# Mamba's opening chain rearranged, and the experts' choices made chunk by chunk

## The chip, the cores and the metric

The kernel runs on one core of one Trainium2 chip. The time is device microseconds of one execution. The engines are named as in the profile: PE (TensorE), DVE (VectorE), ACT (ScalarE), POOL (GpSimd) and SP (SyncE, which only issues DMAs and loads registers). Each engine works through its own queue in order, and semaphores tie the queues together.

## The reference

The input is an image tensor of 2 x 256 x 32 x 32 in f32. Four layers follow each other.

```python
x = x + mamba_blocks(group_norm(x))      # layer 0: two Mamba blocks, 16 states, 512 inner channels
x = involution(x)                        # layer 1: 7x7 taps, two convolutions, softmax, weighted shifts
t = tokens(x)
t = t + linear_attention(layer_norm(t))  # layer 2
t = t + experts(layer_norm(t))           # 16 experts, the best 2 of each token
t = t + softmax_attention(layer_norm(t)) # layer 3
t = t + experts(layer_norm(t))
```

A Mamba block projects 256 channels to 512, convolves along the tokens with four taps per channel, and computes a step size delta = softplus(dt @ dt_w + dt_b). Then it runs, for each of 512 channels and 16 states, h = exp(delta * A) * h + delta * B * x over 1024 tokens. The sum over the states of h * C, plus D * x, is gated and projected back. In the experts' layers each token's gate logits (16) give its two best experts and their softmax weights; each expert is silu(z w1) * (z w2), times w3.

## The kernel before

There are 2048 tokens, in 4 chunks of 512 (`NCH`) and 16 tiles of 128 (`NT`). A planner orders the whole program: it takes the instructions in the order in which the Python code issues them as their priority, models each one's duration, and lets a later instruction go ahead of an earlier one on the same engine where the earlier one's inputs are not ready by its model. So the order of the Python code is a priority, not the order on the engine.

**Mamba** (`layer0`, lines 564 to 644). `GroupNorm.image` normalises one image: `bn_stats` on DVE (L207), a PE product with a block matrix that averages over the eight channels of a group (L210, L219), small DVE steps (L212 to L217), a square root on ACT (L146), and four DVE instructions that rewrite `x` (L225). `Mamba.load` loads a block's weights and makes 16 diagonal 128 x 128 matrices of the convolution's taps (L257); `load_rest` makes four more of D (L277). `Mamba.front(j)` computes what a chunk needs before its scan: PE projection (L300), PE convolution by the diagonals (L327), `xd`, `ct`, then `dt` on PE (L370) and softplus in pieces on ACT (Abs L375, Exp L383, Ln L386) and on DVE or POOL (L377 to L401). The very first front (`alone=True`) has nothing beside it and uses DVE. There are eight units (two blocks, four chunks). `scan(j)` runs 16 states. Per state, POOL multiplies `du` by a broadcast row of B (L450, two products of 128 x 1024, into six buffers `h`), ACT makes exp(delta * A) in PSUM (L457), and DVE scans (L461, four of 128 x 512). PE transposes the result (L429), and DVE adds it into `ya` (L438). The next unit's front, the rest of the last one (`back`) and the next block's loads are issued in between at paced slots, 63 to a scan (`paced`). PSUM has two banks `mm`, three `da` and three `ht`.

**Experts.** `Gate.chunk(j, psum)` is called when a chunk of four tiles has left the attention before: it normalises the tiles, writes them to DRAM (`zd`), transposes them and computes the logits (L1297, L1301). After the last chunk `route` (L1330) chooses the two best experts of all 16 tiles at once (L1348 to L1354, on 128 x 256), counts, and gives each of 2 x 2048 choices a slot in groups of 128 rows of one expert. It then makes `expert` (which expert a group belongs to, L1404), `used` (how many groups there are, L1406), and by one-hot products on PE (L1433) the inverse of the slots, `target` and `source` (L1440, L1442). `experts` loads `used` into registers (L1477). Per group, POOL gathers 128 rows of `zd` by `source` (L1484), SP reads the expert's number (L1489) and issues its weights, 1536 KB (L1491); PE multiplies (L1514, L1528), and POOL scatters the result (L1534). 38 groups always run; more run under a condition on `used`.

Of the kernel before, what the change touches and what calls it, by code (L numbers as in the profile page):

```python
# [10 lines left out]
F32 = mybir.dt.float32  # L11
I32 = mybir.dt.int32
# [7 lines left out]
P = 128  # L20
# [4 lines left out]
C = 256  # L25
# [40 lines left out]
class Net:  # L66
# [30 lines left out]
    def counters(self, const):  # L97

        nc = self.nc
        self.rows = const.tile([P, NROWS], F32, name="rows_sb")  # L100
        nc.sync.dma_start(self.rows, self.rows_dram.partition_broadcast(P))
# [38 lines left out]
    def row(self, name):  # L140
        at, w = _ROWS[name]
        return self.rows[:, at : at + w]
# [38 lines left out]
class GroupNorm:  # L181
# [18 lines left out]
    def image(self, b):  # L200
# [8 lines left out]
        ps = self.psum.tile([P, TC], F32, tag="mm", name=f"gn_ps{b}")  # L209
# [8 lines left out]
        ps = self.psum.tile([P, TC], F32, tag="mm", name=f"gn_ps2{b}")  # L218
# [11 lines left out]
class Mamba:  # L230
# [14 lines left out]
    def load(self):  # L245
# [8 lines left out]

        self.taps = wpool.tile([P, NDC * 4, P], F32, tag="taps", name=f"{m}_taps")
        for i in range(NDC * 4):
            nc.vector.tensor_scalar_mul(  # L257
                self.taps[:, i, :], net.ident, net.col(f"{m}_conv_w", i)
            )
# [3 lines left out]
        self.state = wpool.tile([P, NS, NDC], F32, tag="state", name=f"{m}_state", bufs=2)  # L263

    def load_rest(self):
# [10 lines left out]
        for dc in range(NDC):  # L276
            nc.vector.tensor_scalar_mul(self.skip[:, dc, :], net.ident, net.col(f"{m}_D", dc))  # L277
# [6 lines left out]
    def front(self, j, alone=False):  # L284
# [83 lines left out]
        for dc in range(NDC):  # L368
            ps = self.ps_mm.tile([P, TC], F32, tag="mm", name=f"{m}_dt_{j}_{dc}")
# [35 lines left out]
    def scan(self, j, before, between):  # L405
# [38 lines left out]
        for n in range(NS):  # L444
# [3 lines left out]
            for g in range(NDC // G):  # L448
                h = scanp.tile(half, F32, tag="h", name=f"{m}_h_{j}_{n}_{g}", bufs=6)
                nc.gpsimd.tensor_mul(  # L450
# [113 lines left out]
def layer0(net, x, x_dram, m1, m2, load_image, taps, conv_dram, lg):  # L564
# [5 lines left out]
    with (  # L570
# [15 lines left out]
        norm = GroupNorm(net, wpool, ps_mm, x)  # L586
        blocks[0].load()
        load_image()
# [6 lines left out]
        units = [(m, j) for m in blocks for j in range(NCH)]  # L595
        for _ in units[0][0].front(0, alone=True):
            pass
        norm.image(1)
        before, done = iter(()), []
        aside = taps.make(ps_mm, conv_dram)  # L600
        for u, (m, j) in enumerate(units):
            steps = [(b, Mamba.GATED, 0, 35) for b in done]
            fronts = []
            for a, k in units[u + 1 : u + 2]:
                if k == 0:
                    a.load()
                fronts.append(a.front(k))
            rest = m.load_rest() if u and j == 0 else iter(())
# [26 lines left out]
            before = m.scan(j, before, paced(63, steps))  # L635
# [527 lines left out]
def softmax_attention(net, t, combine, then, scores):  # L1163
# [5 lines left out]
    with (  # L1169
# [56 lines left out]
        for i in range(NT):  # L1226
# [40 lines left out]
            if i % TPC == TPC - 1:  # L1267
                then(i // TPC, ps_mm)


class Gate:


    def __init__(self, net, layer, t, gate_w, pool, dram):
# [5 lines left out]
        self.weight = pool.tile([P, 2, NT], F32, tag="weight", name=f"{layer}_weight")  # L1280
        self.yd = net.nc.dram_tensor(f"{layer}_yd", (2 * T, C), F32, kind="Internal").ap()

    def chunk(self, j, psum):
        net, nc, layer, pool = self.net, self.net.nc, self.layer, self.pool
        z = pool.tile([P, TPC, C], F32, tag="z", name=f"{layer}_z_{j}")
        tiles = [z[:, i, :] for i in range(TPC)]
        net.norm_rows(tiles, [self.t[:, j * TPC + i, :] for i in range(TPC)])
        nc.sync.dma_start(
            self.zd[j * TC : (j + 1) * TC, :].rearrange("(i p) c -> p i c", p=P), z
        )  # L1290
        zt = pool.tile([P, NCC, TC], F32, tag="gzt", name=f"{layer}_gzt_{j}", bufs=1)
        for cc in range(NCC):
            nc.scalar.copy(zt[:, cc, :], net.transposed(psum, tiles, cc, "mm"))
        ps = psum.tile([P, TC], F32, tag="mm", name=f"{layer}_g_{j}")
        for i in range(TPC):
# [6 lines left out]
            self.logits[:, j * TPC : (j + 1) * TPC, :],  # L1302
            ps[:, : TPC * NE].rearrange("p (i e) -> p i e", e=NE),
            net.row(f"{layer}_gate_b").unsqueeze(1).to_broadcast([P, TPC, NE]),
        )

# [23 lines left out]
def route(net, one, ps_mm, pr, weight):  # L1330
# [10 lines left out]
    belowb = net.below.unsqueeze(1).to_broadcast(sh)  # L1341

    hot = [one.tile(sh, F32, name=f"hot{k}") for k in range(2)]
# [363 lines left out]
```

## Time and profile before

| | us |
|---|---|
| median of 3 runs (2205.85 to 2215.26) | 2212.17 |
| the profiled execution's own time | 2216.64 |
| its span | 2214.9 |
| busy in the span: PE, DVE, ACT, POOL | 1907.6, 1416.1, 963.5, 1007.1 |

The page's strips cut the span into 40 slices of 55.4 us, one digit of busy tenths for each. A line of the timeline gives start and length in us, engine, source line, operation, the tiles written and read, and the count; square brackets hold idle time of the engine just before and what ended it. A line of the groups ends in busy us and mean ns of one, then idle us before. A line of waits reads: who waited, for whom, us in total, times, the longest.

### The profile page before, as it was taken

How to read it: one execution, taken by the hardware profiler on the slowest of the kernel's cores; microseconds unless marked ns; L12 is line 12 of the kernel's file. 1: busy time of each engine (PE TensorE's matmuls, PEld its weight loads, DVE VectorE, ACT ScalarE, POOL GpSimd, SP SyncE). 2: the span in 40 equal slices, each digit the busy share in tenths (PEclk: the TensorE clock that was granted, in tenths of full speed). 3: DMA queues.
4: the chain of work that ended last, by engine and by line, in shares of the span. 5: the costliest groups of instructions: out<-in, count | busy, mean ns of one | idle time of the engine just before them, and what ended most of it. 6: DMA issues, size and time to landing. Idle time of an engine off the chain costs nothing.

```text
span 2214.9 us, 27264 instructions
## 1 busy us (share of the span) xinstructions
PE 1907.6 (86%) x9652; PEld 1349.1 (61%) x9652; DVE 1416.1 (64%) x2184; ACT 963.5 (44%) x1611; POOL 1007.1 (45%) x688
## 2 busy tenths in 40 slices
PE   5779888798988989788999999949999599949996
PEld 2445554555555555555556555638999467649995
DVE  5999999999999989999204376662222443342223
ACT  4576765767766767754212264411111132311111
POOL 1687694968768596885024240003333000023331
PEclk8879878897998979799999999969999899969997
DMA  2121121111212111220030100027999300049998
GB/s 105 36 61 49 36 65 32 42 51 40 70 33 66 32 49 38 58 68 24 5 67 1 48 15 0 20 75 258 334 323 346 102 3 17 20 173 332 329 329 295
DMA packets 90483, 224.16 MB, mean 101 GB/s; under 512 B 35451, under 2 KB 51712, under 8 KB 79716
## 3 DMA queue, kind: packets, MB, share of 16 engines
q1 hardware_dynamic: 77620, 198.58, 26.9%
q0 software_dynamic: 7728, 19.15, 2.8%
q10 hardware_dynamic: 4992, 4.59, 0.7%
q8 instruction: 81, 1.33, 0.2%
q14 instruction: 62, 0.51, 0.1%
HBM read 204.88 MB, written 19.37 MB: 101 GB/s over the span
## 4 chain that ended last, share of the span: by engine, by line
PE 34%; DVE 23%; issue 19%; POOL 11%; ACT 8%; DMA 4%; POOLq 0%; ACTq 0%; DVEq 0%; SPq 0%
DVE m_h L461 11%; DVE m_ya L438 6%; PE acc L746 3%; POOL x L1484 3%; PE m_ht L429 3%; POOL l_yd L1534 3%; PE early_acc L746 3%; PE av L1260 3%; PE sc L1234 2%; DMA l_yd<-y,target 2%; PE h L1083 2%; ACT m_da L457 2%; POOL m_h L450 2%; PE m_xd_ps L342 2%; PE w L1092 1%
## 5 line engine op out<-in xcount | busy, mean ns | idle before, releaser
L450 POOL TENSOR_TENSOR m_h<-m_du,m_b 128x1024 f32<-128x1024 f32 x256 | 602.4, 2375 | 254.8 <-PE m_ht L429 106.9
L429 PE MATMUL m_ht<-ident,m_h 128*128 128x128 f32 x2048 | 370.0, 311 | 140.5 <-DVE m_ya L438 87.5
L429 PEld LDWEIGHTS m_ht<-ident,m_h 128*128 128x128 f32 x2048 | 268.3, 158 | 333.7 <-DVE m_ya L438 117.8
L457 ACT ACTIVATE m_da<-m_delta,m_aneg 128x512 f32<-128x512 f32 x512 | 349.3, 690 | 229.3 <-DVE m_h L461 228.7
L1484 POOL DMA_INDIRECT x<-l_zd,source x82 | 83.5, 1018 | 580.7 <-DVE source L1442 222.4
L438 DVE SCALAR_TENSOR_TENSOR m_ya<-m_ht,m_ct,m_ya 128x512 f32<-128x512 f32 x448 | 319.4, 732 | 28.1 <-PE m_ht L429 27.4
L461 DVE TENSOR_TENSOR_SCAN m_h<-m_da,m_state,m_h 128x512 f32<-128x512 f32 x256 | 318.3, 1269 | 14.8 <-ACT m_da L457 7.6
L461 DVE TENSOR_TENSOR_SCAN m_h<-m_da,m_h 128x512 f32<-128x512 f32 x256 | 302.9, 1208 | 15.8 <-ACT m_da L457 13.6
L1514 PEld LDWEIGHTS h<-xts,we 128*128 128x128 f32 x2528 | 298.6, 194 | 9.4 <-issue 5.5
L1514 PE MATMUL h<-xts,we 128*128 128x128 f32 x2528 | 300.0, 278 | 3.4 <-issue 2.5
L1521 DVE TENSOR_TENSOR hid<-hid,h 128x512 f32<-128x512 f32 x79 | 54.3, 688 | 265.2 <-PE h L1514 265.2
L1520 ACT ACTIVATE hid<-h 128x512 f32<-128x512 f32 x79 | 47.2, 597 | 380.7 <-issue 319.0
L1528 PE MATMUL o<-we,hid 128*128 128x256 f32 x632 | 150.6, 380 | 3.4 <-DVE hid L1521 1.9
L1534 POOL DMA_INDIRECT l_yd<-y,target x79 | 80.1, 1015 | 134.2 <-DVE y L1533 128.5
L1528 PEld LDWEIGHTS o<-we,hid 128*128 128x128 f32 x632 | 113.7, 190 | 17.4 <-DVE y L1533 2.8
L327 PE MATMUL m_conv<-m_pre,m_taps 128*128 128x512 f32 x240 | 115.1, 603 | 5.7 <-ACT m_gate L487 5.6
L746 PE MATMUL early_acc<-x,early 128*98 128x448 f32 (+21 forms) x308 | 97.4, 448 | 0.0
L746 PE MATMUL acc<-x,pair 128*98 128x416 f32 (+21 forms) x308 | 94.0, 453 | 0.0
L1533 DVE COPY y<-o 128x256 f32<-128x256 f32 x79 | 33.6, 425 | 70.3 <-PE o L1528 70.3
L746 PEld LDWEIGHTS acc<-x,pair 128*98 128x98 f32 x308 | 47.8, 167 | 40.2 <-issue 34.8
L517 PE MATMUL m_out<-m_out_sb,m_xs 128*128 128x256 f32 x256 | 71.9, 411 | 0.0
L483 PE MATMUL m_g<-x,m_gate_sb 128*128 128x512 f32 x128 | 66.2, 627 | 2.0 <-ACT m_gate L487 1.0
(317 smaller groups left out, 2843.6 us busy)
## 6 DMA issues: line engine op xcount, KB each, us to landing
we<-in_l_experts_dram SPq DMA_DIRECT2D x82, 1536.0 KB
m_b<-m_bd SPq DMA_DIRECT2D x128, 256.0 KB
w<-in_l_w_dram SPq DMA_DIRECT2D x21, 256.0 KB
l_zd<-l_z SPq DMA_DIRECT2D x8, 512.0 KB
l_yl<-l_yd SPq DMA_DIRECT2D x10, 256.0 KB
l_yl<-l_yd ACTq DMA_DIRECT2D x10, 256.0 KB
early<-taps SPq DMA_DIRECT2D x7, 343.0 KB
pair<-taps SPq DMA_DIRECT2D x7, 343.0 KB
```

Of the source, the lines that this page charges most:

```text
L327: nc.tensor.matmul(ps, lhsT=self.taps[:, dc * 4 + k, :], rhs=pre[:, dc, k : k + TC], start=(k == 0), stop=(k == 3),)
L429: nc.tensor.transpose(ps[:, dc * P : (dc + 1) * P], hs[dc // G][:, dc % G, i * P : (i + 1) * P], net.ident,)
L438: nc.vector.scalar_tensor_tensor(ya[:, i, :], ps, c, ya[:, i, :], ALU.mult, ALU.add)
L450: nc.gpsimd.tensor_mul(h, du[:, g * G : (g + 1) * G, :], b.unsqueeze(1).to_broadcast(half))
L457: nc.scalar.activation(da, delta[:, dc, :], AF.Exp, scale=self.aneg[:, i : i + 1])
L461: nc.vector.tensor_tensor_scan(h, da, h, 0.0 if first else state[:, n, dc : dc + 1], ALU.mult, ALU.add)
L517: nc.tensor.matmul(a, lhsT=y[:, dc, i * P : (i + 1) * P], rhs=self.out_sb[:, dc, :], start=False, stop=(dc == NDC - 1),)
L746: nc.tensor.matmul(a[:, lo - 16 * k : hi - 16 * k, co : co + n], lhsT=lhsT, rhs=self.x[:, kc, b, lo - r0 : hi - r0, ci : ci + n], start=(u ...
L1484: nc.gpsimd.indirect_dma_start(out=x, out_offset=None, in_=zd[:, :], in_offset=bass.IndirectOffsetOnAxis(ap=source[:, g : g + 1], axis=0), ...
L1514: nc.tensor.matmul(ps[:, at], lhsT=w12[:, s, kc, at], rhs=xt[:, kc * P : (kc + 1) * P], start=(kc == 0), stop=(kc == NCC - 1),)
L1528: nc.tensor.matmul(ps[:, :C], lhsT=ht[:, mc * P : (mc + 1) * P], rhs=w[:, 8 + mc, :], start=(mc == 0), stop=(mc == NHC - 1),)
L1534: nc.gpsimd.indirect_dma_start(out=yd[g], out_offset=bass.IndirectOffsetOnAxis(ap=target[:, g : g + 1], axis=0), in_=y, in_offset=None, bo ...
```

## The change

- The 16 tap diagonals are made on POOL, in a generator of their own: for the first block ahead of the second image's load, for the second block at slots 26 to 38 of the third unit's scan (`NCH - 2`). The four D diagonals go to POOL too.
- Both images are normalised ahead of the first front (before, image 1 came after it), and the norm's PSUM tiles come from `ht` instead of `mm`.
- In the first front three of the four `dt` products take `ht` banks.
- In the first unit's scan, state 0's two products run on DVE instead of POOL.
- `Gate.chunk` can take a part of a chunk. In layer 3 the last chunk is issued as three tiles and one. At its end chunk j issues the choice of chunk j - 1 (`choose`), and `route` that of the last. The one-hots of both choices live in one tile `hot`, and `slot` is made by one product and one sum.
- `behind`, `ex`, `expert` and `used` are issued behind the last of the row one-hots on DVE.
- The broadcast `rows` begins at `l2_g2`.

```diff
     def counters(self, const):
-        self.rows = const.tile([P, NROWS], F32, name="rows_sb")
-        nc.sync.dma_start(self.rows, self.rows_dram.partition_broadcast(P))
+        self.rows_from = _ROWS["l2_g2"][0]
+        self.rows = const.tile([P, NROWS - self.rows_from], F32, name="rows_sb")
...
@@ GroupNorm.image
-        ps = self.psum.tile([P, TC], F32, tag="mm", name=f"gn_ps{b}")
+        ps = self.psum.tile([P, TC], F32, tag="ht", name=f"gn_ps{b}")
...
@@ Mamba.load
-        self.taps = wpool.tile([P, NDC * 4, P], F32, tag="taps", name=f"{m}_taps")
-        for i in range(NDC * 4):
-            nc.vector.tensor_scalar_mul(
-                self.taps[:, i, :], net.ident, net.col(f"{m}_conv_w", i)
-            )
...
+    def diagonals(self):
+        self.taps = self.wpool.tile(
+            [P, NDC * 4, P], F32, tag="taps", name=f"{self.m}_taps"
+        )
+        for i in range(NDC * 4):
+            self.net.nc.gpsimd.tensor_scalar_mul(
+                self.taps[:, i, :], self.net.ident, self.net.col(f"{self.m}_conv_w", i)
+            )
+            yield
...
-            nc.vector.tensor_scalar_mul(self.skip[:, dc, :], net.ident, net.col(f"{m}_D", dc))
+            nc.gpsimd.tensor_scalar_mul(self.skip[:, dc, :], net.ident, net.col(f"{m}_D", dc))
...
@@ Mamba.front
-            ps = self.ps_mm.tile([P, TC], F32, tag="mm", name=f"{m}_dt_{j}_{dc}")
+            pool, tag = (self.ps_ht, "ht") if alone and dc else (self.ps_mm, "mm")
+            ps = pool.tile([P, TC], F32, tag=tag, name=f"{m}_dt_{j}_{dc}")
...
@@ Mamba.scan
-                nc.gpsimd.tensor_mul(
+                (nc.vector if start and n == 0 else nc.gpsimd).tensor_mul(
                     h, du[:, g * G : (g + 1) * G, :], b.unsqueeze(1).to_broadcast(half)
                 )
...
@@ layer0
-        norm = GroupNorm(net, wpool, ps_mm, x)
+        norm = GroupNorm(net, wpool, ps_ht, x)
         blocks[0].load()
+        for _ in blocks[0].diagonals():
+            pass
         load_image()
...
         units = [(m, j) for m in blocks for j in range(NCH)]
+        norm.image(1)
         for _ in units[0][0].front(0, alone=True):
             pass
-        norm.image(1)
...
+            if u == NCH - 2:
+                steps.append((blocks[1].diagonals(), NDC * 4, 26, 38))
...
-            before = m.scan(j, before, paced(63, steps))
+            before = m.scan(j, before, paced(63, steps), u == 0)
...
@@ softmax_attention
-            if i % TPC == TPC - 1:
+            if i == NT - 1:
+                then(NCH - 1, ps_mm, 0, TPC - 1)
+                then(NCH - 1, ps_mm, TPC - 1)
+            elif i % TPC == TPC - 1:
                 then(i // TPC, ps_mm)
...
@@ Gate
+        self.hot = pool.tile([P, 2, NT, NE], F32, tag="hot", name=f"{layer}_hot", bufs=1)
...
-    def chunk(self, j, psum):
+    def chunk(self, j, psum, first=0, end=TPC):
...
+        if end == TPC and j:
+            self.choose(j - 1)
+
+    def route(self, one, psum):
+        self.choose(NCH - 1)
+        return route(self.net, one, psum, self.hot, self.weight)
+
+    def choose(self, j):
+        net, nc, pool = self.net, self.net.nc, self.pool
+        at = slice(j * TPC, (j + 1) * TPC)
+        sh = [P, TPC, NE]
+        belowb = net.below.unsqueeze(1).to_broadcast(sh)
+        pr = self.logits[:, at]
+        tmp = pool.tile(sh, F32, tag="tmp", name=f"{self.layer}_tmp_{j}")
+        e = pool.tile([P, TPC], F32, tag="first", name=f"{self.layer}_first_{j}")
+        for k in range(2):
+            m, hot = self.weight[:, k, at], self.hot[:, k, at]
+            nc.vector.tensor_reduce(m, pr, AX.X, ALU.max)
+            nc.vector.tensor_tensor(tmp, pr, m.unsqueeze(2).to_broadcast(sh), ALU.is_equal)
+            nc.vector.tensor_mul(tmp, tmp, belowb)
+            nc.vector.tensor_reduce(e, tmp, AX.X, ALU.min)
+            nc.vector.tensor_tensor(hot, belowb, e.unsqueeze(2).to_broadcast(sh), ALU.is_equal)
+            if k == 0:
+                nc.vector.scalar_tensor_tensor(pr, hot, -3e38, pr, ALU.mult, ALU.add)
...
@@ route
-    for k in range(2):
-        nc.vector.tensor_mul(tmp, hot[k], place)
-        nc.vector.tensor_reduce(slot[:, k, :], tmp, AX.X, ALU.add)
-    gs = [1, NG, NE]
-    behind = one.tile(gs, F32, name="behind")
...
+    tmp = one.tile([P, 2, NT, NE], F32, name="rtmp")
+    nc.vector.tensor_mul(tmp, hot, place.unsqueeze(1).to_broadcast([P, 2, NT, NE]))
+    nc.vector.tensor_reduce(slot, tmp, AX.X, ALU.add)
...
+    with net.tc.issue_after(last.ins):
+        gs = [1, NG, NE]
+        behind = one.tile(gs, F32, name="behind")
...
@@ experts
-        expert, used, source, target = route(net, one, ps_mm, gate.logits, gate.weight)
+        expert, used, source, target = gate.route(one, ps_mm)
```

## The prediction

> **What bounds the kernel now.** I read the page first: its two strips say which engine fills which stage.
>
> ```profile
> span 2214.9 us, 27264 instructions
> ...
> PE   5779888798988989788999999949999599949996
> ...
> DVE  5999999999999989999204376662222443342223
> ```
>
> Each digit is 55 us. VectorE (DVE) is full from the first slice to about 1060 us (Mamba); then TensorE (PE) is. The 4s in PE's strip at the 27th and 36th digits are the routing ahead of each expert stage. Second, the timeline of the opening:
>
> ```profile
> 7.82 3.19 DVE L257 TENSOR_SCALAR m_taps<-ident,cols_sb 128x128 f32<-128x128 f32 x16
> 10.93 0.87 DVE L277 TENSOR_SCALAR m_skip<-ident,cols_sb 128x128 f32<-128x128 f32 x4
> 11.71 0.15 DVE L212 COPY gn_gm<-gn_ps 128x2 f32<-128x2 f32 x1
> ...
> 15.63 9.92 PE L300 MATMUL m_in<-x,m_in_sb 128*128 128x512 f32 x16 [1.13 <-DVE x L225]
> ...
> 51.32 5.46 POOL L450 TENSOR_TENSOR m_h<-m_du,m_b 128x1024 f32<-128x1024 f32 x1 [24.80 <-DVE m_du L401]
> ...
> 57.32 1.21 DVE L461 TENSOR_TENSOR_SCAN m_h<-m_da,m_h 128x512 f32<-128x512 f32 x1
> ...
> 65.19 8.72 DVE L225 TENSOR_SCALAR x<-x,gn_gm,gn_rs 128x512 f32<-128x512 f32 x4
> ```
>
> L212's input is there at 8.6 (PE's L210 ends), yet DVE makes 20 diagonals first. The first scan starts at 57.32, and image 1's norm then stands in the middle of the scans: its four L225 take 8.72 us where image 0's four take 1.91. Third, DVE's groups and waits from 60 to 1060 us:
>
> ```profile
> L257 DVE TENSOR_SCALAR m_taps<-ident,cols_sb 128x128 f32<-128x128 f32 x16 | 8.8, 618 | 0.0
> L225 DVE TENSOR_SCALAR x<-x,gn_gm,gn_rs 128x512 f32<-128x512 f32 x4 | 8.7, 2238 | 0.0
> L277 DVE TENSOR_SCALAR m_skip<-ident,cols_sb 128x128 f32<-128x128 f32 x4 | 6.0, 1548 | 0.0
> ```
> ```profile
> DVE m_ya L438 <- PE m_ht L429: 27.4, 32, 2.7
> DVE m_h L461 <- ACT m_da L457: 21.2, 23, 2.5
> DVE m_h L461 <- POOL m_h L450: 9.1, 8, 2.2
> ```
>
> DVE waits 60 us in these 1000, so 94% of what leaves it there is on the path. Last, layer 2's routing (layer 3's has the same rows 467 us later):
>
> ```profile
> 1471.06 0.42 DVE L1348 TENSOR_REDUCE l_weight<-l_logits 128x16 f32<-128x256 f32 x1
> ...
> 1476.09 0.42 DVE L1356 TENSOR_TENSOR both<-hot,hot 128x256 f32<-128x256 f32 x1
> ...
> 1481.37 0.92 DVE L1397 TENSOR_TENSOR behind<-end,iota 1x752 f32<-1x752 f32 x1
> 1482.56 0.92 DVE L1402 TENSOR_REDUCE ex<-behind 1x47 f32<-1x752 f32 x1
> ...
> 1486.01 3.75 SPq L1491 DMA_DIRECT2D we<-in_l_experts_dram  x4
> ...
> 1497.02 1.26 POOL L1484 DMA_INDIRECT x<-l_zd,source  x1 [187.81 <-ACT w0t L1140]
> ...
> 1503.99 0.69 PE L1498 MATMUL xt<-ident,x 128*128 128x128 f32 x2 [3.52 <-DMA x<-l_zd,source]
> ```
>
> DVE runs back to back from the logits to `source`; the weights are asked for 11 us ahead of the gather, and PE then waits for the gather, which needs 7 us beside the weights' transfers.
>
> **The change part by part.**
> *Opening.* (a) Taps and skip go to GpSimd: 4.06 us leave DVE ahead of L212, of which 3.1 (8.6 to 11.71) are wait. GpSimd has no such row at 128x128; its nearest are a copy of 128x128 at 0.30 us and its tensor-scalar L883, 32x112, at 0.55 us (median). I take L883 stretched to 128, 0.63, as the same operation: 20 end at 5.1 + 12.6 = 17.7, ahead of the convolution (25.4 before). But they now run beside L215-L217 and L225, and two such engines lock each other out (0.54 became 2.24 above), so I count 2.5 of the 3.1; ends 0 and 3.1. (b) From there PE's chain is unmoved but earlier: first Abs (L375) at 38.24 - 2.5 = 35.7. With four PSUM banks (three of the transposes' banks, free until the first scan) ScalarE runs 4 Abs (0.69), load, 4 Exp (0.63), load, first Ln (0.70): 44.2; the tables are loaded three times from L383 to L457, not five (1.28 each). DVE's earlier steps fit beneath. Its last twelve sums and products run at a pitch of 0.60: 51.4; one wait behind a GpSimd product, 2.0 (L399 took 2.71 once, not 0.69): 53.4. (c) The two products of state 0 now run on DVE: L1105, 128x1024, is 1.23 us; the first before the scans: first scan at 54.6, not 57.3. (d) Image 1's norm goes ahead of the front, into DVE's idle 5.9 us before L314; without that cover it costs its 1.9 us. The nine scans that ended at 78.4 then need 9 x 1.17 + 1.2 (second product) + 0.7 (one L438) + 1.0 (half a lock wait) = 13.4, ending at 68.0: 10.4 saved, 9.4 at nine tenths. Ends: 4 (norm no earlier, three lock waits) and 13 (no lock).
> The Trainium skill (SBUF, "Who interferes with whom") says a DVE instruction with two SBUF inputs and a GpSimd one that reads SBUF exclude each other for the whole instruction. L225 and L399 agree; taken strictly, each product of state 0 could stand behind a whole GpSimd product of 2.35 us, which would make the gain about 2 us smaller.
> *Second block's diagonals.* 8.8 + 6.0 = 14.8 us leave DVE; at 85% (the 94% less some reordering) 12.6. GpSimd gains 16 x 0.63 = 10.1 us in unit 2 (315 to 442 us), where it is busy 90.4 of 127, and 2.5 in unit 4; most of it idles in products that wait for a free `h` buffer, so these cost nothing. Queued behind them are L450's products, for which the scans wait. Without that cover (at 400 to 450 us it is busy 49.3 of 50) 12.6 comes back. Ends: 2 and 14.8. DVE's scans read one operand from PSUM and take 1.21 us whether GpSimd works or not.
> The Trainium skill (GPSIMD Engine Reference, "Key points") speaks against this: elementwise work is about twice as fast on DVE. Here DVE's mean of 618 ns is no better than the 0.63 that I take, so by the trace the move is free; if the rule set the time, 14.8 us would return as twice that on an engine with 36 us idle in unit 2.
> *Routing, each layer.* The eleven choice steps go from 256 columns (0.457 pitch, 5.0) to 64 for the last chunk only (L1301: 0.22, pitch 0.26, 2.9): 2.2. Two pairs for `slot` (1.8) become one of 512 columns (0.69 + 0.69, 1.45): 0.4. `behind` to `used` leave the chain between L1381 and L1393: 1.5. The last row one-hot so ends 4.1 earlier, at 1490.4; then the four moved steps (2.1) and the three short ones of the slots' inverse (0.6) share DVE: `used` at 1493.1, and `source` up to 0.9 late. Behind `used` on SP's queue stand all weight loads: 1.85 us later, as before (1484.16 to 1486.01), 1495.0. The first expert is 1.57 MB; transfers began 1.4 us after the issue and ran at 430 GB/s (windows of 2 us): 1500.0, or 1501.9 with 0.79 MB of gathers between. The gather, issued at 1493.8, lands by 1501 and its turn is done by 1502. Before, the first expert product began at 1505.19: 3.2 to 5.2 saved; I take 4.0. If four loads share the rate evenly, the first lands at 1511: 5.8 lost.
> *Layer 3's last chunk* in 3 + 1 tiles: PE's 6 transposes (1.6) and 12 gate products (2.8) run while tile 15 is normalised, but its copy waits for the single `gzt` buffer: logits at about 1936.4, not 1938.0: 1.6 (ends 0 and 3.5). With 4.0: 5.6.
> *Earlier chunks' choices*: 33 x 0.26 = 8.6 us on DVE in each attention, where DVE is busy 103 of 170 and 80 of 175 us and PE 157 and 168; hidden but for 0.5 in all; uncovered 17. The shorter `rows` transfer, and layer 3's last `zd` write, now two on SP's queue well ahead of the weight loads, are off the path.
> Sum: 9.4 + 12.6 + 4.0 + 5.6 - 0.5 = 31.1. The profiled execution took 2216.64 us (span 2214.9), 0.2% above the median of 2212.17; 31.1 of it is 1.40%, so 2181 on the median.
>
> **The rivals.**
> 1. *Another engine takes DVE's place.* PE is busy 20 to 24 of 25 us in Mamba's windows at a granted clock down to 0.6, and DVE already waits 27.4 us for its transposes. If a quarter of the Mamba terms comes through (5.5 of 22): 14.6 saved, 2198. Against it: those waits are 6% together.
> 2. *The weights arrive last*, shared among four loads: 5.8 lost in layer 2, 4.2 in layer 3: 31.1 - 9.6 - 10.0 = 11.5 saved, 2201. For it: they are now behind `used`; against: one queue issues them in order.
> 3. *Slower: GpSimd's diagonals block.* L883's longest took 2.17 us behind DVE. If all 20 of block two's took that, in the saturated half of a unit, 43.4 us would come onto its products: 31.1 - 43.4 = -12.3, 2224. It decides from 31.1 / 20 = 1.6 us each with no slack left; against it stand the median and 36 us of slack.
>
> **How the numbers follow.** Forecast 0.66, rival 1 0.15, rival 2 0.13, rival 3 0.06. Best ends: 13 + 14.8 + 5.2 + 8.7 = 41.7, 2170; the planner orders the whole program anew, worth an estimated 8 us either way (an eighth of DVE's 60 us of waits): 2162. Upwards the range takes in rivals 1 and 2: 2203. A change under 0.5% (11 us) can't be told from none here. Faster by more: 0.66 + two thirds of rival 1 + about half of rival 2, 0.83; within 0.5% the rest of these, 0.11; slower 0.06.
>
> **What would show it.** Right: L212 near 8.7; first scan near 55, nine done by 68; no L257 or L277 on DVE and GpSimd rows of 0.3 to 0.7 us there; three table loads from L383 to L457; first expert product 4 us sooner after the logits. Wrong: DVE's waits for PE or POOL grow past 80 us from 60 us to Mamba's end; GpSimd's diagonals over 1.6 us; PE's first expert product waiting for `we`.

## The result, and the profile after

| | before | after |
|---|---|---|
| median, us | 2213.24 (4 runs, 2205.85 to 2215.26) | 2188.19 (4 runs, 2185.56 to 2189.62) |
| ratio to before | | 0.9891 [0.9866, 0.9916] |
| the profiled execution | 2216.64 | 2188.29 |
| its span | 2214.9 | 2186.6 |

The change saves 25.0 us by the medians and 28.3 us between the two profiled spans; the profiled execution of before (2216.64 us) was slower than all four of its timed ones, so gains that are read against its trace come out too large by a few us. The forecast was 31.1 us saved and 2181 us. Direction and range were right. The parts were not: Mamba gave more than its terms, and the routing nothing.

The page's strips of the kernel after:

```profile
span 2186.6 us, 27311 instructions
...
PE   6888898898978888788999989949999599859996
...
DVE  6999998999999999899005475752222544432223
```

As before, DVE fills Mamba (now to about 1030 us) and PE the rest. PE's low slices at the routings, the 27th (4) and the 36th (4 before, 5 now), have hardly changed.

The timeline of the opening after: DVE and PE lines, then POOL's.

```profile
8.59 0.16 DVE L216 COPY gn_gm<-gn_ps 128x2 f32<-128x2 f32 x1 [0.74 <-PE gn_ps L214]
11.88 1.97 DVE L229 TENSOR_SCALAR x<-x,gn_gm,gn_rs 128x512 f32<-128x512 f32 x4
12.43 6.20 PE L309 MATMUL m_in<-x,m_in_sb 128*128 128x512 f32 x8 [2.33 <-DVE x L229]
...
21.03 1.91 DVE L229 TENSOR_SCALAR x<-x,gn_gm,gn_rs 128x512 f32<-128x512 f32 x4
51.53 1.22 DVE L461 TENSOR_TENSOR m_h<-m_du,m_b 128x1024 f32<-128x1024 f32 x1
53.26 1.22 DVE L472 TENSOR_TENSOR_SCAN m_h<-m_da,m_h 128x512 f32<-128x512 f32 x1
54.40 2.40 DVE L461 TENSOR_TENSOR m_h<-m_du,m_b 128x1024 f32<-128x1024 f32 x1
56.72 7.90 DVE L472 TENSOR_TENSOR_SCAN m_h<-m_da,m_h 128x512 f32<-128x512 f32 x7
65.77 1.22 DVE L472 TENSOR_TENSOR_SCAN m_h<-m_da,m_h 128x512 f32<-128x512 f32 x1
```
```profile
6.14 9.59 POOL L269 TENSOR_SCALAR m_taps<-ident,cols_sb 128x128 f32<-128x128 f32 x15
15.72 2.34 POOL L286 TENSOR_SCALAR m_skip<-ident,cols_sb 128x128 f32<-128x128 f32 x4
```

The copy of the group means stands at 8.59, not 11.71; image 1's rewrite takes 1.91 us at 21.03, not 8.72 in the scans; the first scan starts at 53.26, not 57.32; nine scans end at 66.99, not 78.38. The second product of state 0 takes twice the first's time beside POOL. A diagonal costs 0.6 us on POOL.

DVE's waits after, from 60 us to Mamba's end (us in total, times, longest):

```profile
DVE m_h L472 <- POOL m_h L461: 19.2, 13, 4.9
DVE m_h L472 <- ACT m_da L468: 19.0, 23, 2.5
DVE m_ya L449 <- PE m_ht L440: 17.5, 26, 2.2
DVE m_xs L516 <- PE m_y L512: 1.9, 3, 1.3
```

In all 57.6 us, against some 60 before; those for PE fell from 27.4 to 17.5, those for POOL rose from 9.1 to 19.2, 4.9 of it at once.

Layer 2's routing and the first expert tiles after, on DVE, SP, POOL and PE:

```profile
1440.46 0.23 DVE L1325 TENSOR_TENSOR l_logits<-l_g,rows_sb 128x64 f32<-128x64 f32 x1 [5.16 <-PE l_g L1321]
1440.72 0.22 DVE L1348 TENSOR_REDUCE l_weight<-l_logits 128x4 f32<-128x64 f32 x1
...
1460.05 0.92 DVE L1469 TENSOR_TENSOR behind<-end,iota 1x752 f32<-1x752 f32 x1
...
1462.32 0.19 DVE L1465 TENSOR_SCALAR source<-target 128x47 int32<-128x47 int32 x1
```
```profile
1463.08 3.75 SPq L1527 DMA_DIRECT2D we<-in_l_experts_dram  x4
```
```profile
1463.39 1.27 POOL L1520 DMA_INDIRECT x<-l_zd,source  x1 [184.27 <-ACT w1t L1156]
```
```profile
1470.81 0.69 PE L1534 MATMUL xt<-ident,x 128*128 128x128 f32 x2 [4.42 <-DMA x<-l_zd,source]
1472.66 0.66 PE L1534 MATMUL xt<-ident,x 128*128 128x128 f32 x2 [1.16 <-DMA x<-l_zd,source]
1475.15 0.66 PE L1534 MATMUL xt<-ident,x 128*128 128x128 f32 x2 [1.83 <-DMA x<-l_zd,source]
1475.60 5.08 PE L1550 MATMUL h<-xts,we 128*128 128x128 f32 x32
1483.25 0.41 PE L1534 MATMUL xt<-ident,x 128*128 128x128 f32 x2 [2.57 <-DMA x<-l_zd,source]
1483.50 0.60 PE L1564 MATMUL o<-we,hid 128*128 128x256 f32 x2
```

`source` comes 21.86 us after the logits, not 25.15: 3.3 saved. But the weights are asked for 0.3 us ahead of the first gather, not 11, and PE's queue holds the turns (PE's transpositions of a tile's gathered rows into `xt`) of three tiles ahead of the first product, and the fourth's ahead of the second. Before, it ran one turn, the first product, one turn, and so on (DVE's logits and `source`, then PE):

```profile
1470.80 0.22 DVE L1301 TENSOR_TENSOR l_logits<-l_g,rows_sb 128x64 f32<-128x64 f32 x1 [5.16 <-PE l_g L1297]
1495.95 0.19 DVE L1442 TENSOR_SCALAR source<-target 128x47 int32<-128x47 int32 x1
...
1505.19 5.87 PE L1514 MATMUL h<-xts,we 128*128 128x128 f32 x32 [0.52 <-issue]
1510.89 0.38 PE L1498 MATMUL xt<-ident,x 128*128 128x128 f32 x2
```

Each turn waits for its gather, and the first product starts 35.14 us after the logits; before, 34.39.

By place in the two profiled executions (first `ya` copy of a unit, logits, span end):

| up to | gained there | prediction |
|---|---|---|
| start of unit 1 | 15.2 | 9.4 |
| start of unit 7 | 15.1 more | 12.6 |
| layer 2's logits | 0.0 | -0.5 |
| the end | -2.0 | 9.6 |

### The profile page after: what moved, and what is told of

Same layout as the page of the kernel before. It is cut to its first block, busy times and chain, and to the rows that moved or that the text cites. A ratio compares the mean times of both kernels' runs of the same rounds, so it can differ in the third digit from the quotient of the medians.

```text
span 2186.6 us, 27311 instructions
## 1 busy us (share of the span) xinstructions
PE 1894.0 (87%) x9652; PEld 1335.5 (61%) x9652; DVE 1400.3 (64%) x2210; ACT 959.2 (44%) x1610; POOL 1028.9 (47%) x726
## 4 chain that ended last, share of the span: by engine, by line
PE 32%; DVE 22%; issue 19%; POOL 11%; ACT 10%; DMA 5%; POOLq 0%; SPq 0%; DVEq 0%; ACTq 0%
DVE m_h L472 11%; DVE m_ya L449 6%; PE acc L762 3%; POOL x L1520 3%; POOL l_yd L1570 3%; PE m_ht L440 3%; PE early_acc L762 3%; PE av L1276 3%; ACT m_da L468 2%; PE sc L1250 2%; DMA l_yd<-y,target 2%; POOL m_h L461 2%; PE h L1099 2%; PE m_xd_ps L351 1%; PE w L1108 1%
## 5 line engine op out<-in xcount | busy, mean ns | idle before, releaser
L461 POOL TENSOR_TENSOR m_h<-m_du,m_b 128x1024 f32<-128x1024 f32 x254 | 594.5, 2364 | 196.0 <-PE m_ht L440 95.8
L440 PE MATMUL m_ht<-ident,m_h 128*128 128x128 f32 x2048 | 361.2, 305 | 119.4 <-DVE m_ya L449 83.9
L440 PEld LDWEIGHTS m_ht<-ident,m_h 128*128 128x128 f32 x2048 | 259.5, 154 | 317.8 <-DVE m_ya L449 112.7
L449 DVE SCALAR_TENSOR_TENSOR m_ya<-m_ht,m_ct,m_ya 128x512 f32<-128x512 f32 x448 | 320.2, 733 | 18.4 <-PE m_ht L440 17.5
L472 DVE TENSOR_TENSOR_SCAN m_h<-m_da,m_state,m_h 128x512 f32<-128x512 f32 x256 | 318.7, 1271 | 14.7 <-POOL m_h L461 8.7
L309 PE MATMUL m_in<-x,m_in_sb 128*128 128x512 f32 x128 | 68.8, 663 | 9.8 <-ACT m_pre L313 6.9
```

The source lines that it names most:

```text
L309: nc.tensor.matmul(ps, lhsT=self.in_sb[:, kc, mc * P : (mc + 1) * P], rhs=self.xt[:, kc, tok], start=(kc == 0), stop=(kc == NCC - 1),)
L440: nc.tensor.transpose(ps[:, dc * P : (dc + 1) * P], hs[dc // G][:, dc % G, i * P : (i + 1) * P], net.ident,)
L449: nc.vector.scalar_tensor_tensor(ya[:, i, :], ps, c, ya[:, i, :], ALU.mult, ALU.add)
L461: (nc.vector if start and n == 0 else nc.gpsimd).tensor_mul(h, du[:, g * G : (g + 1) * G, :], b.unsqueeze(1).to_broadcast(half))
L472: nc.vector.tensor_tensor_scan(h, da, h, 0.0 if first else state[:, n, dc : dc + 1], ALU.mult, ALU.add)
```

## The experiments

Ratios are to the kernel before on the same chip, whose medians were 2205.3 to 2210.3 us.

**Which half holds the gain.** First, the Mamba parts alone, and the routing parts (with the shorter `rows`) alone, each put on the kernel before.

```diff
 # mamba_only: of the change, only
+    def diagonals(self):              # taps and skip on gpsimd
...
+        norm.image(1)                 # ahead of front
...
+            pool, tag = (self.ps_ht, "ht") if alone and dc else (self.ps_mm, "mm")
...
+                (nc.vector if start and n == 0 else nc.gpsimd).tensor_mul(
...
 # routing_only: of the change, only
+        self.rows_from = _ROWS["l2_g2"][0]
...
+    def choose(self, j):              # and the split last chunk, slot in one
...
+    with net.tc.issue_after(last.ins):   # behind, ex, expert, used
```

> The kernel before with the Mamba parts of the change alone (GpSimd's diagonals in both blocks, both norms ahead of front, the norms' products and three of the delta products in the ht banks, the state-0 product of the first unit on VectorE); Gate, routing and the rows' load as before. Theory A: the whole gain of the change lies in Mamba (scans end 30.3 us sooner in the changed kernel), and routing as changed gives nothing or loses about 2 us: 2183 to 2187 us, no slower than the changed kernel. The prediction's terms (opening 9.4, second block 12.6, routing 9.6): 2191 to 2195 us, slower than the changed kernel by the routing's gain. The rows' load, which the changed kernel cuts short, is not cut here; if the cut is worth something in the opening, it shows as a later first scan than 53.3 us.

> The kernel before with the other half of the change alone: rows cut to those that are used, choices chunk by chunk, the last chunk in two, the expert's numbers behind the row products. Theory A (lost head start): the logits of layer 3 come about 3 us sooner by the split chunk and source 3.3 us sooner in each layer, and the first expert products lose it again: within 2 us of the kernel before plus the cut of the rows' load, which is worth 0 to 3 us in the opening: 2209 to 2215 us. The prediction's terms (4.0 in layer 2, 5.6 in layer 3, and nothing from the rows): 2202 to 2205 us.

Measured: mamba_only 2185.26 us, ratio 0.9884 [0.9860, 0.9909]; routing_only 2212.59, ratio 1.0002 [0.9981, 1.0024]. The whole gain is Mamba's; the routing as changed is worth nothing. mamba_only's first scan starts at 53.2 us with the long `rows`, so their cut is worth nothing in the opening.

**Where the routing's gain went.** Two kernels each put one thing back into the changed kernel.

```diff
 # expert_early: the weights' numbers early again
+    behind = one.tile(gs, F32, name="behind")    # then ex, expert, used
...
     n = 2 * NT
     sloti = one.tile([P, n], I32, name="sloti")
...
-    with net.tc.issue_after(last.ins):
...
-        behind = one.tile(gs, F32, name="behind")
...
 # turn_behind: PE's order only; opened[g] is the first product of tile g
-                    if g + 1 < end:
+                    if g + 1 < end and g < PART:
+                        with net.tc.issue_after(opened[g]):
+                            xt = turned(g + 1, loaded[g + 1][0])
+                    elif g + 1 < end:
                         xt = turned(g + 1, loaded[g + 1][0])
```

> The changed kernel with one thing put back: behind, ex, expert and used are made ahead of slot's conversion again, as in the kernel before, so that the weights of the first expert tiles are asked for ahead of the gathers; everything else of the change stays. Theory A (lost head start): in the changed kernel SP issues the first weights 0.6 us after source is ready, and weights and gathers share the DMA engines; PE's turns of the rows wait 10.0 us for x in layer 2 and 14.7 us in layer 3, against 3.5 and 8.2 in the kernel before. With the early issue these waits fall back to about 3.5 and 8.2; the expert chain's four small instructions come back into the way of source (about 2 us by their durations), so source is later by some 2 us than in the changed kernel, and the first expert product sooner after source. Net 2 to 5 us a layer: 2178 to 2184 us against 2188.2 of the changed kernel. Rival B (PE's order): the changed kernel has PE turn three tiles' rows ahead of the first product; this kernel has the old order too (rows 0, product 0, rows 1), so it predicts the same here, and is told apart by turn_behind. Rival C (nothing to win: the gathers' own latency sets the first product): source later by 2 us a layer and all behind it too, 2190 to 2193 us.

> The changed kernel with PE's order of before in the expert loop's first tiles (the turn of the next tile's rows is issued behind the first product of the present one), and the weights still asked for as late as in the changed kernel. Rival B (PE's order): the first product of layer 2 stands at 1475.60 us behind the third tile's turn at 1475.15; without it it starts when the weights and the first rows are there. If the order is what costs, the first product comes about 4 us sooner in layer 2 and 3 in layer 3, the later ones too, 2180 to 2182 us. Theory A (lost head start): the volume that weights and gathers move together sets when the third and fourth tiles can be done, whatever stands first on PE: the first product comes sooner by up to 4 us, but the fourth by less than 1.5, and the time stays at 2186 to 2190 us.

Measured: expert_early 2174.68 us, 0.9840 [0.9813, 0.9866]; turn_behind 2174.81, 0.9840 [0.9814, 0.9865]. Both are faster than the change, whose ratios were 0.9891 and 0.9893. turn_behind asks for the weights as late as the changed kernel does and still has the whole gain, so theory A, that the lost head start alone costs, is refuted. expert_early's PE order is that of before too, as its expectation says. PE's timeline of turn_behind in layer 2:

```profile
1467.99 0.69 PE L1534 MATMUL xt<-ident,x 128*128 128x128 f32 x2 [4.45 <-DMA x<-l_zd,source]
1469.20 5.57 PE L1550 MATMUL h<-xts,we 128*128 128x128 f32 x32 [0.52 <-DVE xts L1538]
1474.61 0.38 PE L1534 MATMUL xt<-ident,x 128*128 128x128 f32 x2
```

One gather is waited for; the second lands under the first product. Both gained more than had been expected. One reason may be the fourth turn: in the change it stands ahead of the second product and waits 2.6 us (layer 3: 3.2).

The remaining combination is early weights with three turns first.

```diff
 # turns_ahead, on expert_early; ins is the third tile's last transpose
+            if first == 0:
+                ahead[1] = turned(1)
+                loaded[2] = load(2)
+                third, ins = turn(2, loaded[2][0])
...
-                    hid = up(g, xt, loaded[g][1])
+                    with net.tc.issue_after(ins) if g == 0 else nullcontext():
+                        hid = up(g, xt, loaded[g][1])
+                    if g == 0:
+                        ahead[2] = copied(2, third)
```

> expert_early (weights asked for as early as in the kernel before, 2174.7 us) with PE made to turn the first three tiles' rows ahead of the first product, as the changed kernel does. Theory B (the order alone costs): the first product stands behind the third gather again, 3 to 4 us later after source in each layer than expert_early's 9.2: 2181 to 2187 us. Theory B2 (the order costs only where the weights come late, since only then do gathers land late beside them): the third gather lands within 2 us of the first, 2175 to 2179 us.

The changed kernel ran beside it:

> The changed kernel itself, on the chip of the three runs beside it, as their base: about 2188 us (2185 to 2190). If it stands at 2175 here, the gain of turn_behind and expert_early was one of the chip and not of the order.

Measured on that chip: the changed kernel 2183.18 us (0.9893 [0.9871, 0.9915]), turns_ahead 2180.89 (0.9876 [0.9854, 0.9898]; its six runs lie between 2173.9 and 2182.9). PE's timeline of turns_ahead:

```profile
1466.37 0.62 PE L1534 MATMUL xt<-ident,x 128*128 128x128 f32 x2 [3.38 <-DMA x<-l_zd,source]
1467.55 0.66 PE L1534 MATMUL xt<-ident,x 128*128 128x128 f32 x2 [0.55 <-DVE xts L1542]
1468.72 0.69 PE L1534 MATMUL xt<-ident,x 128*128 128x128 f32 x2 [0.52 <-DVE xts L1542]
1469.21 9.28 PE L1554 MATMUL h<-xts,we 128*128 128x128 f32 x64
```

With the weights early the gathers of the second and third tile are there when PE comes to them; its turns wait 0.5 us for DVE's copies, not 1.2 and 1.8 for DMAs. The steps of all variants, from their profiled executions (us):

| | logits to `source`, layer 2 | `source` to first product, layer 2 / 3 | layer 2's logits to the end |
|---|---|---|---|
| before | 25.15 | 9.24 / 8.86 | 744.1 |
| mamba_only | 25.14 | 9.33 / 8.72 | 744.5 |
| the change | 21.86 | 13.28 / 12.05 | 746.1 |
| the change, second chip | 21.86 | 13.53 / 12.22 | 746.0 |
| routing_only | 21.87 | 13.44 / 12.23 | 746.8 |
| expert_early | 22.59 | 9.15 / 9.01 | 737.5 |
| turn_behind | 21.86 | 9.80 / 9.28 | 734.6 |
| turns_ahead | 22.60 | 11.15 / 11.11 | 736.7 |

By these executions late weights together with the turns ahead cost some 10 us from the logits to the end, and either alone costs none of it. Two things limit this reading. The five kernels that keep the routing of before (before, mamba_only and three of the next experiments) need 741.7 to 746.5 us for this stretch, so a few us between two rows say nothing. And the profiled execution of turns_ahead was its fastest (2173.9 us): its median lies only 2.3 us below the change, at the lower end of theory B (2181 to 2187) and above B2 (2175 to 2179). With late weights the order is what costs, as turn_behind shows. Whether it costs with early weights too is open, and so is how the 10 us divide between the third and the fourth turn, which stands further back in turns_ahead than in the change.

**The opening's parts.** Three kernels put parts of the Mamba half on the kernel before. The last two also take the norms' products from `ht`, and diagonals_only moves the D diagonals too.

```diff
 # image_first
+        norm.image(1)
         for _ in units[0][0].front(0, alone=True):
             pass
-        norm.image(1)
 # opening_no_diag: that, and
+            pool, tag = (self.ps_ht, "ht") if alone and dc else (self.ps_mm, "mm")
...
+                (nc.vector if start and n == 0 else nc.gpsimd).tensor_mul(
 # diagonals_only: instead of these, both blocks'
-            nc.vector.tensor_scalar_mul(
+            self.net.nc.gpsimd.tensor_scalar_mul(
                 self.taps[:, i, :], net.ident, net.col(f"{m}_conv_w", i)
```

> The kernel before with one line moved: image 1's norm ahead of the first front, not behind it. Its four products took 8.72 us in the middle of the first scans, beside GpSimd; ahead of the front the same four should take about 1.9 to 2.2 us, and part of that in time in which VectorE waits anyway. Theory (the lock, and the place on the path): 6.8 us from the shorter products, and up to 8.7 if they are hidden whole; PE's late transposes in the first unit (6.0 us of waits) may go with it: 2200 to 2204 us. Rival (the norm was no load there, the scans wait for GpSimd's products instead): the two products of state 0 on GpSimd then set the first scans, within 3 us of the kernel before: 2207 to 2210 us.

> The kernel before with the opening's other parts (both norms ahead of front, four PSUM banks for the transposed sums of delta, the two products of state 0 on VectorE), all diagonals still on VectorE. The prediction's terms: 9.4 less the 2.5 of the diagonals, 6.9: 2203 us. By the changed kernel's trace the opening is worth 15.2 up to the second unit, of which 3.2 is the earlier m_in: 12.0, 2198 us. If the opening's part is not kept to the end it is under 4: 2207 or more.

> The kernel before with the diagonals of both blocks made on GpSimd and the norms' small products in the ht banks, and nothing else: image 1's norm still in the scans, two PSUM banks for delta, GpSimd's product for state 0, routing as before. The prediction's terms: 2.5 in the opening and 12.6 in the second block, 15.1: 2195 us against 2210.3 of the kernel before. By the changed kernel's trace: 3.2 in the opening (m_in's start), 4.9 in unit 2, 7.1 in unit 3 with the skip, 2.8 behind it: 18.0, 2192 us. If the gains behind unit 2 belong to another part of the change (the new order of the whole), it stops at 8 us: 2202.

Measured: image_first 2200.04 us (0.9968 [0.9951, 0.9984]), opening_no_diag 2194.43 (0.9950 [0.9932, 0.9967]), diagonals_only 2190.68 (0.9933 [0.9916, 0.9950]), beside 2205.32 of before: 5.3, 10.9 and 14.6 us. The first is a little under the 6.8 us of its theory, the second lies between the 6.9 of the prediction's terms and the 12.0 of the trace, and the third near the 15.1 of the prediction's terms.

Where in the kernel these gains lie is another matter. Up to the start of unit 1 the profiled executions gain 8.1 (image_first), 11.3 (opening_no_diag) and 9.7 us (diagonals_only) on before's; all together, in the change, 15.2. In the traces they overlap. The times do not settle it: by the medians 10.9 and 14.6 make 25.5, and mamba_only, which has both, gained 25.0; by the means of the same runs 13.0 and 16.1 stand beside 23.4. In the kernel before, DVE waits for PE's transposes in unit 0 as this view of its waits from 60 to 187 us shows:

```profile
DVE m_ya L438 <- PE m_ht L429: 6.0, 5, 2.0
```

It is 2.3 us in image_first, 2.7 in diagonals_only, 1.6 in opening_no_diag and in the change: each part takes some of the same wait away. In diagonals_only image 1's four products still stand in the scans, but took 6.1 us and not 8.72.

**The second block's diagonals.** In the changed kernel they were put back on DVE, and, separately, made three times each on POOL (the same values written again).

```diff
 # dve2 (skip likewise)
+        eng = self.net.nc.gpsimd if self.m == "m1" else self.net.nc.vector
...
-            self.net.nc.gpsimd.tensor_scalar_mul(
+            eng.tensor_scalar_mul(
 # triple (skip likewise)
+            for _ in range(1 if self.m == "m1" else 3):
+                self.net.nc.gpsimd.tensor_scalar_mul(
```

> The changed kernel with the second block's 20 diagonals back on VectorE, at the same places in the program; the first block's stay on GpSimd. The prediction's term for them is 12.6 us: 2200 to 2201. Rival (the gain of the later units came with the new order of the whole program: the kernel with the opening's parts alone already takes 122.0 us in unit 4 with its skip diagonals on VectorE, against 127.7 in the kernel before): the diagonals cost less than half of that, 2188 to 2194 us.

> The changed kernel with each of the second block's 20 diagonals made three times on GpSimd (the same values written again): 1.8 us for each in place of 0.6, above the 1.6 from which the prediction's slower rival says that the change loses. Rival 3 as written (no slack): 40 more instructions of 0.6 us, 24 us, come onto the scans, 2212 us, no faster than the kernel before. If GpSimd's slack of the whole unit covers them as the prediction had it: 2188 to 2192 us. By the trace of the changed kernel (a block in unit 2, after which VectorE waits; skip in unit 4 hidden): 14 to 19 us, 2202 to 2207.

Measured: dve2 2188.41 us, 0.9910 [0.9886, 0.9935], 5.2 above the change on the same chip (the intervals overlap); triple 2200.33, 0.9965 [0.9950, 0.9980], 17.2 above it. The groups of dve2 from 190 us on, with their mean ns:

```profile
L270 DVE TENSOR_SCALAR m_taps<-ident,cols_sb 128x128 f32<-128x128 f32 x16 | 6.7, 482 | 0.0
L288 DVE TENSOR_SCALAR m_skip<-ident,cols_sb 128x128 f32<-128x128 f32 x4 | 1.3, 372 | 0.0
```

The same 20 instructions that took 14.8 us of DVE in the kernel before take 8.0 here. The four of skip on DVE's timeline, before and in dve2:

```profile
634.31 4.93 DVE L277 TENSOR_SCALAR m_skip<-ident,cols_sb 128x128 f32<-128x128 f32 x3
654.62 1.10 DVE L277 TENSOR_SCALAR m_skip<-ident,cols_sb 128x128 f32<-128x128 f32 x1
```
```profile
611.78 0.67 DVE L288 TENSOR_SCALAR m_skip<-ident,cols_sb 128x128 f32<-128x128 f32 x3
626.95 0.65 DVE L288 TENSOR_SCALAR m_skip<-ident,cols_sb 128x128 f32<-128x128 f32 x1
```

In the changed kernel POOL makes the 16 taps in one block, and DVE then waits (POOL's line and DVE's):

```profile
332.77 9.33 POOL L269 TENSOR_SCALAR m_taps<-ident,cols_sb 128x128 f32<-128x128 f32 x16
```
```profile
344.46 2.34 DVE L472 TENSOR_TENSOR_SCAN m_h<-m_da,m_h 128x512 f32<-128x512 f32 x2 [4.87 <-POOL m_h L461]
```

Against the change on the same chip (where this wait is 4.85 us) DVE is busy 5.9 us longer in unit 2 of dve2, but does not have that wait: the unit is 1.1 us longer (129.6, 128.4), unit 4 0.1. Most of the rest by which the two traces differ up to unit 7 lies in units in which no diagonals are made (2.4 us each in units 1 and 6). So their move is worth about 5 us in this kernel by the medians, of which 1.2 can be placed; it is not 12.6. In diagonals_only, 14.6 less the 9.7 gained up to unit 1 leaves 4.9, though that mixes a median with traces. And the 15.1 us that the change's trace shows between units 1 and 7 are no measure of the diagonals: opening_no_diag, with all of them on DVE, shows 13.5 there.

In triple, POOL made 37 of the 48 diagonals of unit 2 in one piece, and DVE waited (POOL's line and DVE's):

```profile
330.14 21.54 POOL L270 TENSOR_SCALAR m_taps<-ident,cols_sb 128x128 f32<-128x128 f32 x37
```
```profile
354.02 2.34 DVE L474 TENSOR_TENSOR_SCAN m_h<-m_da,m_h 128x512 f32<-128x512 f32 x2 [17.07 <-POOL m_h L463]
```

Unit 2 took 142.8 us, not 128.4: 14.3 of the some 19 us that POOL had more to do in it came through to the scans. The 36 us of slack that POOL has over that unit in the kernel before cover little of a block. The time is just under the 2202 to 2207 us worked out from the trace. Yet triple is still faster than the kernel before at 1.8 us a diagonal, past the rival's 1.6.

The last kernel spreads the block, on turn_behind.

```diff
-                steps.append((blocks[1].diagonals(), NDC * 4, 26, 38))
+                steps.append((blocks[1].diagonals(m), NDC * 4, 26, 50))
...
+            with self.net.tc.issue_after(at.product) if at else nullcontext():
+                self.net.nc.gpsimd.tensor_scalar_mul(
```

> The kernel of turn_behind, in which the second block's 16 diagonals on GpSimd are also spread: each is put behind the h product traced last, one to three between two products, over two thirds of what is left of the unit. In the changed kernel they stand in one block (332.77 to 342.10 us), VectorE then waits 4.87 us for the next h product, and the unit gains 4.9 of the 8.8 us that left VectorE. Theory (the block empties the scans' supply): without the block that wait goes, VectorE's waits for GpSimd from 60 to 1040 us fall from 19 us to about 14, and the time is some 4 to 5 us less than turn_behind's 2174.8: 2169 to 2172 us. Rival (GpSimd has no slack there, wherever they stand): the 10 us of diagonals come onto its products anyway, the wait is cut into smaller ones of the same sum, 2174 to 2177 us.

Measured: 2174.64 us, 0.9866 [0.9844, 0.9887] of a before at 2205.32; in us no less than turn_behind, in ratio not faster either. DVE's waits in unit 2, of turn_behind and of spread:

```profile
DVE m_h L472 <- POOL m_h L461: 5.4, 2, 4.8
```
```profile
DVE m_h L474 <- POOL m_h L462: 6.5, 5, 1.9
```

The long wait is gone and its sum is not. Unit 2 is 2.1 us shorter in spread (126.5, 128.6) and unit 3 1.9 longer (121.9, 119.9). That is the rival of this run, diagonals that come onto POOL's products in a block or spread.

turn_behind and expert_early (35.5 and 35.6 us below the kernel before beside them) are faster than both kernels; their times do not tell them apart, and spread adds nothing to the first.

## Why the prediction was right and wrong

**The opening: 9.4 predicted, 15.2 by the trace up to unit 1.** The steps held one by one. Group means copied at 8.59 (predicted 8.6 to 8.7), first Abs at 35.36 (35.7), three table loads (three), POOL's 20 diagonals done at 18.1 (17.7) at 0.63 us on average (0.63), first scan at 53.26 (54.6), nine scans done at 66.99 (68.0). So 10.4 was 11.4. The step that failed is the factor of nine tenths, for which the prediction gives no reason: it takes 1.0 us off behind the nine scans. Instead 3.8 us more came up to unit 1, while DVE's wait for PE's transposes in unit 0 fell from 6.0 to 1.6. By the medians the opening is worth still more: dve2, which has all of it and the second block's diagonals on DVE, is 21.1 us below the kernel before on its chip, and the routing gave nothing. Where the part behind unit 1 lies is not shown. The lock wait counted for the first rewrite (0.6) did not come: beside POOL's diagonals the four took 1.97 us, not 1.91.

On that lock, the Trainium skill (SBUF, "Who interferes with whom") has a DVE instruction with two SBUF inputs and a POOL one that reads SBUF exclude each other. The second product of state 0 took 2.40 us beside POOL's, the first 1.22, which fits: 1.2 us of wait, for which the prediction had 1.0. Of the two lines that the prediction names for the rule, L399 reads two tensors; L225 reads one tensor and two columns, and no run here separates what made it 2.24 us beside POOL's products.

**The second block's diagonals: 12.6 predicted, about 5 by the medians.** The failed step is "14.8 us leave DVE". That is their time in the order of the kernel before, in which 6 of the 20 met POOL's products and took 1.1 to 2.5 us each, the others about 0.3. It is no accident of one execution: the 16 taps took 8.8 us again in routing_only, image_first and opening_no_diag, and the four of skip 6.0 in the first two. But it goes with the order: skip took 3.6 us in opening_no_diag, and in dve2 the 20 took 8.0. Nor did the cover hold, POOL's busy and idle time of which the prediction said that "most of it idles in products that wait for a free `h` buffer, so these cost nothing": the 16 stood in one block of 9.33 us, DVE waited 4.87 behind it, and spread could not win that back. Rival 3's mechanism, a block that empties the scans' supply, is real, at under a third of its price (0.63 us each, not 2.17).

The Trainium skill (GPSIMD Engine Reference, "Key points") says that elementwise work is about twice as fast on DVE. Here a diagonal took 0.20 us on DVE ahead of the scans (3.19 for 16) and 0.63 on POOL, three times as long, and the kernel with all of them on POOL was still 14.6 us faster (diagonals_only). The rule gives the duration; it does not tell which engine to use.

**Routing, 4.0 a layer: nothing came.** `source` did come 3.3 us sooner, as predicted (3.2). The failed step is the one after: "The gather ... lands by 1501 and its turn is done by 1502", that is, the first product stands behind one gather as before. It kept PE's old order. In the new one the product stands behind three gathers, which land beside the weights. Rival 2 had the weights arrive last and the two layers 10.0 us slower than before. They came out 2.0 slower in the traces, and by the gathers: no product of the change's first tiles waited for `we`, while the turns waited 10.0 us for `x` in layer 2 and 14.7 in layer 3 (before: 3.5 and 8.2). With the order put back the first product comes 31.66 us after the logits, 2.7 sooner than before and not 4.0, and the whole from the logits to the end gains 9.5 on before's execution (744.1 to 734.6), against 9.6 predicted for the two layers, with a few us of uncertainty. The size was about right, the premise was not.

**Layer 3's last chunk: 1.6 predicted, 3.1 measured.** Layer 3's last logits come 33.3 us after those of the third chunk in the kernel before (441.8 and 408.5 us after layer 2's `source`) and 30.2 after (444.1 and 413.9). It was within its ends of 0 and 3.5.

**Earlier chunks' choices, -0.5**: layer 2's logits come some 519.3 us after unit 7's start in both kernels. Hidden, as said.

**Rival 1**, another engine in DVE's place, did not come: DVE's waits went from some 60 to 57.6 us, under the 80 named. (PE was busy 16 to 24 of 25 us in Mamba's windows, not 20 to 24.)

In sum Mamba was put at 22.0 and gave 25.0 by the medians (mamba_only), 30.3 by the two profiled executions; the routing was put at 9.1 and gave nothing. The two errors have opposite signs, and within Mamba an opening that gave more stands beside a second block that gave less. That the forecast missed by only 7.2 us is in part luck.

## What to carry to other kernels

When an edit makes one input of a queue later, read again what stands in front of the first instruction on the engine that uses it: an order made by a planner does not stay, and two more gathers ahead of the first product, and one ahead of the second, ate here what two layers had won. The duration of an instruction that another engine locks out (here 0.25 to 2.46 us for the same diagonal) goes with the order of that one kernel; cost its removal by its free duration and its locked one as two ends. Small work on the engine that feeds the bound can be paid in large part, however idle that engine is over the stage: here 14.3 of some 19 us, with six buffers between the two engines and 36 us of idle time, and spreading the block won nothing.

## What the runs showed of the hardware

The same program differs by unit between executions. The changed kernel's profiled executions on two chips, in units 1 and 3 (the columns are the window, its length, and busy time of PE, PEld, DVE, ACT and POOL with counts, then granted clock, DMA share, GB/s):

```profile
172.54:300.25 127.71, 108.40 (x503) 71.12 (x502) 118.08 (x136) 88.90 (x132) 96.72 (x53) 0.87 0.15 46
427.94:551.14 123.20, 107.33 (x502) 70.55 (x502) 115.82 (x133) 88.73 (x133) 95.67 (x53) 0.88 0.15 48
```
```profile
171.20:296.42 125.22, 104.14 (x503) 68.19 (x502) 118.13 (x136) 88.83 (x131) 97.09 (x53) 0.89 0.15 47
424.86:544.83 119.97, 103.71 (x502) 69.37 (x502) 115.52 (x133) 88.73 (x133) 95.44 (x53) 0.90 0.16 49
```

DVE is as busy in both. PE is busy 3.6 to 4.3 us longer at a clock lower by 0.02, and the unit is 2.5 to 3.2 us longer. DVE's wait for PE's transposes is 4.5 us against 1.9 in unit 1, 3.1 against 0.7 in unit 3. Unit 5 of the kernel before, 128.1 us at 0.84, took 125.1 at 0.88 in routing_only, whose Mamba is untouched. So some of the 15.1 us that the trace shows between units 1 and 7 is probably no work removed, only slow stretches of PE that fell elsewhere; a gain of 3 us in one unit can't be read from one pair of traces. What places these stretches was not tried. Nor was it expected that the same diagonals on DVE can take anything from 0.25 us (the shortest in opening_no_diag) to 2.46 us (the longest there) by whether POOL runs a product beside it.
